# Four edits to the order of a graph kernel: weight sums, a load, attention's additions, a copy at the end

## The chip, the cores and the metric

The kernel runs on one core of a Trainium2 chip. The metric is the device time of one execution in microseconds (us), the median of several runs. Times inside an execution come from one profiled execution and count from its first instruction.

Engines are named as the profile names them: PE (TensorE) multiplies matrices, PEld is its loading of weights, DVE is VectorE, ACT is ScalarE, POOL is GpSimd, and SP is the engine that issues nearly all transfers (SyncE).

## What is computed

Two layers on x of shape (16, 1024, 256), with one adjacency matrix of 1024 x 1024, all in float32. Cut to what matters:

```python
# layer 0, per batch: attention whose queries come from a weighted adjacency
c_adj = mean over channels of x                       # (B, N)
diff  = c_adj[:, None, :] - c_adj[:, :, None]
A     = abs(abs(sigmoid(diff) - 0.5) - 0.5) * 2.0
Wg    = adj[None] * (A + transpose(A)) * 0.5
g     = relu(einsum('bcn,bnm->bcm', fea, Wg) * para)  # queries
k, v  = x @ kv_w                                      # 4 heads of 64
out   = softmax(q k^T * scale) v
x     = layernorm(x + out)
# layer 1, per batch: two graph convolutions
h = relu(x @ w1_loop + adj @ (x @ w1_neigh) + b1)
h = relu(h @ w2_loop + adj @ (h @ w2_neigh) + b2)
x = layernorm(x + (x + h) * 0.5)
```

## The kernel before

The order of all instructions is written out by hand: each engine executes its instructions in the order in which `run()` (from line 1363) issues them, and semaphores make an engine wait where data or a buffer isn't ready.

**Batches overlap.** While batch b has its attention (`Attention`), the queries of batch b+1 are prepared (`Queries`, from batch 2 on `FastQueries`), the first convolution of batch b-1 is multiplied (`c1`), and the second of batch b-2 (`c2`). From batch 2 on, the two convolutions share their products with the adjacency (`Joined`), and those, the queries and the keys use seven products of half size in place of eight, from sums of blocks that VectorE and GpSimd form beforehand. Such sums of the weights are formed once, stored to DRAM, and loaded again in each batch.

**Row buffers.** Nearly all tiles of 128 x 1024 come from one pool with the tag "row" and 31 buffers (`ROWS`, `row_tile`). The 32nd tile waits until an earlier one is read for the last time.

**The start.** `load_weights` (lines 146 to 174) loads the convolution's weights, scales them on GpSimd, forms the sums of the second layer (`w2_sums`) and then of the first (`w1_sums`), each in a row buffer, and stores them through SP. Batch 0's queries take eight rows of adjacency: `likeness(t)` computes the weight tile wg on ScalarE (lines 574 and 575), `times_adj(t)` multiplies it by the adjacency on VectorE (line 580), and `step(t)` multiplies on TensorE (line 588). In the loop over t, after row 7's weighing, VectorE also turns the next batch's x and three blocks of the adjacency (line 1406), and subtracts adjacency blocks (`adj_sums`, line 234).

**The middle of a batch, b = 2 to 14.** `att.both_units(1, ...)` computes scores (line 724) and outputs `av` (line 770) of the second pair of heads. Before its outputs, `before_convolution` puts loads on SP: `fetch("00", "10")`, two adjacency rows, `fetch(2, 3)` (four loads of 512 KB of stored adjacency sums), and `c1.load_t1()` (line 984). GpSimd then forms `both.left` (lines 1281 to 1284; from the second on they read t1) and `q.left` (lines 628 to 631).

`both.run` (from line 1293) takes the products of the joined convolutions in the order 1, 2, 6, 7, 5, 4, 3; each is eight TensorE instructions. Work of other parts is put between them: `between[n]` is issued after product n, and after product 4 behind `block_sums` (lines 1079 to 1083). Before the edit `between[1]` holds two `likeness` and `q.right(0)` (four subtractions, lines 641 to 644), `between[2]` holds `att.add_pairs(0, 1)` (denominators, lines 812 to 818, then for each pair a multiplication, an addition and a reduction, lines 821, 823 and 824, and a join of the sums), and `between[4]` two `times_adj`. VectorE's addition `uT` (line 1334) follows product 4; the last layer's small products (line 1092, `seventh_part`) need it. They come in the order 1, 2, 6, 5, 7, then the second half of product 3, then 4 and 3. VectorE's lines 1107, 1114, 1121 and 1096 take their results, and line 1357 that of product 3. Then `q.step(0)` begins on TensorE (line 669), in the PSUM banks that these results leave.

**The end.** `ending` (from line 1171) computes the last batch's second convolution tile by tile: `products` (lines 1185 and 1187), `deviations` (VectorE and GpSimd: residual, statistics, line 1196 on) and `leave` (GpSimd's lines 1204 and 1205, ScalarE's line 1207, then the store). The last quarter of the adjacency products is copied to uT by ScalarE (line 1246), behind `leave` of tile 4.

Of the kernel before, what the change touches and what calls it, by code (L numbers as in the profile page):

```python
# [18 lines left out]
def kernel(  # L19
# [126 lines left out]
    def load_weights():  # L146
        nc.sync.dma_start(out=w1l_sb, in_=w1_loop.rearrange("(cc p) f -> p cc f", p=P))
        nc.sync.dma_start(out=w1n_sb, in_=w1_neigh.rearrange("(cc p) f -> p cc f", p=P))
        nc.sync.dma_start(out=w2l_sb, in_=w2_loop)
        nc.sync.dma_start(out=w2n_sb, in_=w2_neigh)  # L150
        nc.sync.dma_start(out=b1_sb, in_=b1.rearrange("(p o) -> p o", o=1))
        nc.sync.dma_start(out=b2_sb, in_=b2.rearrange("(o f) -> o f", o=1).to_broadcast([P, C]))

        for w in (w2l_sb, w2n_sb, b2_sb):
            nc.gpsimd.tensor_scalar_mul(w, w, 1.0 / 3.0)
        for w in (w1l_sb, w1n_sb):
            nc.gpsimd.tensor_scalar_mul(w, w, LIFT)
        t = row_tile("w2_sums")
        (b11, b12), (b21, b22) = ((w[:, ts(0, P)], w[:, ts(1, P)]) for w in (w2n_sb, w2l_sb))
        t1, t2, t3, t4, b2_step = (t[:, ts(n, P)] for n in range(5))  # L160
        nc.gpsimd.tensor_sub(t1, b12, b11)
        nc.gpsimd.tensor_sub(t2, b22, t1)
        nc.gpsimd.tensor_sub(t3, b22, b12)
        nc.gpsimd.tensor_sub(t4, b21, t2)
        nc.gpsimd.tensor_sub(b2_step, b2_sb[:, ts(1, P)], b2_sb[:, ts(0, P)])
        nc.sync.dma_start(out=w2_sums, in_=t[:, 0:5 * P])
        t = row_tile("w1_sums")
        a11, a12, a21, a22 = (w[:, cc, :] for w in (w1n_sb, w1l_sb) for cc in range(NC))
        s1, s2, s3, s4 = (t[:, ts(n, P)] for n in range(4))
        nc.gpsimd.tensor_add(s1, a21, a22)  # L170
        nc.gpsimd.tensor_sub(s2, s1, a11)
        nc.gpsimd.tensor_sub(s3, a11, a21)
        nc.gpsimd.tensor_sub(s4, a12, s2)
        nc.sync.dma_start(out=w1_sums, in_=t[:, 0:FB])
# [168 lines left out]
    def by_node(t):  # L343
        return t.rearrange("p (bn r) -> p bn r", r=S)
# [351 lines left out]
    class Attention:  # L696
# [108 lines left out]
            third()  # L805

        def add_pairs(self, *pairs):
            b, half, n = self.b, FB // S, NJ * len(pairs)
            u0 = NJ * pairs[0]
            pd = bank_psum(f"den_ps_{b}_{u0}")  # L810
            den = pd[:, 0:n * NB]
            nc.tensor.matmul(den, fold.rearrange("p a k -> p (a k)"),
                             self.part[:, u0:u0 + n, :].rearrange("p u k -> p (u k)"), start=True, stop=True)
            den = den.rearrange("p (u s h) -> p u s h", u=n, s=2)
            rden = self.rden[:, u0 * half:(u0 + n) * half].rearrange("p (u h) -> p u h", u=n)
            for s in range(2):
                rows = slice(s * HD, (s + 1) * HD)
                nc.vector.reciprocal(rden[rows], den[rows, :, s, :])
            for pair in pairs:
                o = by_node(self.o.pop(NJ * pair))  # L820
                nc.vector.tensor_mul(o, o, self.rden[:, ts(pair, NB)].unsqueeze(2).to_broadcast([P, NB, S]))  # L821
                dst = by_node(self.xB[pair])
                nc.vector.tensor_add(dst, dst, o)  # L823
                nc.vector.tensor_reduce(self.sums[:, pair, :], dst, AX.X, ALU.add)  # L824
            if pairs[-1] == NC - 1:
                join(self.sums)

        def add(self, *units):
# [83 lines left out]
    class GraphConv:  # L912
# [258 lines left out]
        def ending(self, dst, quarters, aside, filled):  # L1171
# [68 lines left out]
            leave(*stats)  # L1240
            stats = deviations(4)
            products(5)
            leave(*stats)
            stats = deviations(5)
            self.neighbours(1, fourth[:, 0:half], range(TJ, NT), quarters, slice(half, FB))
            nc.scalar.copy(self.uT[:, FB + half:N], fourth[:, 0:half])
            leave(*stats)
            products(3)
            stats = deviations(3)
            leave(*stats)  # L1250
# [112 lines left out]
    def run():  # L1363
# [59 lines left out]
        for b in range(B):  # L1423
# [29 lines left out]
            if more and not c1:  # L1453
                att.both_scores(0)
                clip()
                NodeSums(q, xb, str(b + 1)).all()
                two_units(0)
                att.both_scores(1)
                for t in range(3):
                    q.load(t)  # L1460
                    q.weigh(t)
                two_units(1)
            elif more and not both:
                att.scores(0)
                att.outputs(0)
                NodeSums(q, xb, str(b + 1)).all()
                kv = KeysValues(b + 1, channel_major(blocked, f"xT_{b + 1}"))
                att.scores(1)
                kv.sums()
                att.add(0)  # L1470
                att.outputs(1)
                for t in (0, TJ):
                    q.load(t)
                c1.inner()
                q.left(nc.gpsimd)
                for t in (0, TJ):
                    q.likeness(t)
                for ij, n in QUARTERS.items():
                    store(n, quarters[ij])
                c1.first(quarters, lambda: (att.add(1), adj_sums(quarters, 1), adj_sums(quarters, 2), weigh_first()))  # L1480
                c1.turn_blocks()
                att.scores(2)
                att.outputs(2)
                for t in (1, TJ + 1):
                    q.load(t)
                    q.likeness(t)
                    q.times_adj(t)
                att.scores(3)
                for t in (2, TJ + 2, 3, TJ + 3):
                    q.load(t)  # L1490
                for t in (2, TJ + 2, 3, TJ + 3):
                    q.likeness(t)
                q.right(1)
                att.add(2)
                att.outputs(3)
            elif more:
                nodes = None

                def sums():
                    nonlocal nodes  # L1500
                    nodes = NodeSums(q, xb, str(b + 1))
                    if c3:
                        c3.squares_aside()
                    c2.load_x()
                    c1.load_inner()

                def summed():
                    c1.inner_sums()
                    if c3:
                        c3.deviation_aside()  # L1510

                def turn_next():
                    nonlocal xT_next
                    xT_next = channel_major(blocked, f"xT_{b + 1}")

                xT_next = None

                def before_convolution():
                    both.fetch("00", "10")
                    for t in (0, TJ):  # L1520
                        q.load(t)
                        q.likeness(t)
                    both.fetch(2, 3)
                    c1.load_t1()

                att.both_units(0, sums, lambda: nodes.turn(), summed=summed)
                nodes.line()
                nodes.row()
                c1.fast_inner(turn_next)
                att.both_units(1, before_convolution, third=lambda: (q.times_adj(0), q.times_adj(TJ)))  # L1530
                both.left(nc.gpsimd)
                q.left(nc.gpsimd, blocked)
                kv = KeysValues(b + 1, xT_next)
                both.fetch(1)
                for t in (1, TJ + 1):
                    q.load(t)
                both.fetch(4, "11")

                def more_weights():
                    for t in (2, TJ + 2, 3, TJ + 3):  # L1540
                        q.load(t)
                        q.likeness(t)
                    if c3:
                        c3.finish_aside(out[b - 3])

                both.run({1: (lambda: q.likeness(1), lambda: q.likeness(TJ + 1), lambda: q.right(0)),
                          2: (lambda: att.add_pairs(0, 1),),
                          4: (lambda: q.times_adj(1), lambda: q.times_adj(TJ + 1)),
                          3: (more_weights, lambda: q.right(1))},
                         last=nc.gpsimd)  # L1550
                c1.turn_blocks()
                if b + 2 < B:
                    c2.sums_aside()
            else:
                att.both_units(0, c1.load_inner, summed=c1.inner_sums)
                c1.fast_inner()
                att.both_units(1, third=lambda: att.add_pairs(0))
# [174 lines left out]
```

## Time and profile before

| | us |
|---|---|
| median of 3 runs | 2148.36 |
| lowest and highest | 2147.54 and 2150.09 |
| the profiled execution, its whole time | 2150.09 |
| the profiled execution, span from first to last instruction | 2148.3 |
| VectorE busy, of the span | 1936.7 (90%) |
| ScalarE busy | 1254.9 (58%) |
| GpSimd busy | 371.1 (17%) |

The profiled execution is itself one of the three runs, the slowest; 1.8 us of its time lie outside the span. In the views, "x8" counts instructions, a group's time is that of all of them, and in brackets stands how long the engine was idle before the group and what ended that wait. A matrix product of 512 columns in float32 is recorded as two instructions. In a windows view each line is a stretch of time, followed by its length, the busy time of PE, PEld, DVE, ACT and POOL with the number of instructions, the granted TensorE clock as a share of full speed, the share of the DMA engines and GB/s.

### The profile page before, as it was taken

The numbers are of one execution on the slowest core, as the hardware profiler recorded it, in microseconds if no ns is written. First come the engines' busy times: TensorE is split into PE (matmuls) and PEld (weight loads), VectorE is DVE, ScalarE is ACT, GpSimd is POOL, SyncE is SP. The second block draws the span as 40 slices with busy tenths as digits, with TensorE's granted clock in tenths as the row PEclk, the third lists the DMA queues.
The fourth block names the chain that finished last, engine by engine and source line by source line (L and its number), as shares of the span: only waits on it lengthen the run. The fifth ranks groups of instructions, "written<-read, shape, count | busy, mean of one in ns | idle before, by whom it ended". The sixth has DMA issues, their size and how long they took to land. (4 is left out here: it accounts for less than half of the span.)

```text
span 2148.3 us, 24753 instructions
## 1 busy us (share of the span) xinstructions
PE 2108.7 (98%) x8360; PEld 994.1 (46%) x8360; DVE 1936.7 (90%) x2212; ACT 1254.9 (58%) x2126; POOL 371.1 (17%) x224
## 2 busy tenths in 40 slices
PE   7999999999999999999999999999999999999998
PEld 4344444535444353444534445354443544445355
DVE  4899999999999899999999999999999999999885
ACT  4654564665747558465675657557475584655523
POOL 2011013122031210313102131120312103121022
PEclk9999999999999999999999999999999999999999
DMA  9388746764758657496664777647586575966454
GB/s 209 90 158 205 153 97 231 152 205 120 157 192 174 210 141 156 169 178 221 140 183 153 152 239 142 217 130 149 208 166 217 122 158 183 181 205 133 145 185 171
DMA packets 688693, 364.98 MB, mean 170 GB/s; under 512 B 550704, under 2 KB 629936, under 8 KB 688560
## 3 DMA queue, kind: packets, MB, share of 16 engines
q1 hardware_dynamic: 688288, 363.07, 65.6%
q8 instruction: 68, 1.11, 0.2%
q14 instruction: 65, 0.53, 0.1%
q10 hardware_dynamic: 272, 0.26, 0.0%
HBM read 305.46 MB, written 57.80 MB: 169 GB/s over the span
## 5 line engine op out<-in xcount | busy, mean ns | idle before, releaser
L745 DVE TENSOR_TENSOR acc<-acc,pr 128x1024 f32<-128x1024 f32 x384 | 481.1, 1253 | 34.3 <-ACT pr L731 0.9
L724 PE MATMUL s<-qT,kT 64*128 64x512 f32 x2048 | 450.8, 594 | 2.3 <-ACT qT L595 2.3
L770 PE MATMUL av<-pr,v 128*64 128x512 f32 x2048 | 447.0, 594 | 0.0
L731 ACT ACTIVATE pr<-s 128x1024 f32<-128x1024 f32 x392 | 390.8, 1115 | 41.7 <-PE s L724 40.9
L724 PEld LDWEIGHTS s<-qT,kT 64*128 64x128 f32 x2048 | 195.8, 187 | 245.0 <-issue 178.1
L770 PEld LDWEIGHTS av<-pr,v 128*64 128x64 f32 x2048 | 144.0, 137 | 297.3 <-issue 267.2
L1290 PE MATMUL hu_ps<-adj,R 128*128 128x512 f32 x480 | 213.6, 592 | 0.0
L374 POOL TENSOR_TENSOR rstd<-rstd,neg_half 128x32 f32<-128x32 f32 x16 | 88.4, 5522 | 617.2 <-DVE rstd L372 617.2
L580 DVE SCALAR_TENSOR_TENSOR wg<-wg,adj 128x1024 f32<-128x1024 f32 x128 | 170.9, 1373 | 26.7 <-ACT wg L575 26.6
L574 ACT ACTIVATE wg<-c_row,c_sums 128x1024 f32<-128x1024 f32 x120 | 139.4, 1162 | 18.9 <-DVE wg L580 17.3
L729 ACT ACTIVATE pr<-s 128x512 f32<-128x512 f32 x240 | 142.3, 702 | 0.6 <-PE s L724 0.6
L575 ACT ACTIVATE wg<-wg 128x1024 f32<-128x1024 f32 x128 | 135.4, 1057 | 4.1
L1290 PEld LDWEIGHTS hu_ps<-adj,R 128*128 128x128 f32 x480 | 89.0, 190 | 100.9 <-issue 97.8
L1290 PE MATMUL hu_ps<-adj,t 128*128 128x512 f32 x240 | 106.8, 597 | 2.8 <-DMA t<-t1d 1.8
L669 PE MATMUL g_ps<-wg,x 128*128 128x512 f32 x224 | 107.7, 593 | 0.0
L669 PE MATMUL g_ps<-T,xB 128*128 128x512 f32 x208 | 107.3, 597 | 0.0
L669 PE MATMUL g_ps<-wg,xB 128*128 128x512 f32 x208 | 106.2, 592 | 0.0
L1313 ACT COPY snap<-hu_ps 128x512 f32<-128x512 f32 x15 | 8.8, 586 | 160.6 <-PE hu_ps L1290 160.6
L1153 POOL TENSOR_TENSOR rstd<-rstd,neg_half 128x8 f32<-128x8 f32 x12 | 19.6, 1638 | 472.6 <-DVE rstd L1152 472.6
L743 DVE TENSOR_TENSOR acc<-pr,pr 128x1024 f32<-128x1024 f32 x64 | 77.9, 1217 | 21.9 <-ACT pr L731 21.9
L1281 POOL TENSOR_TENSOR R<-h 128x512 f32<-128x512 f32 x14 | 20.6, 1472 | 422.5 <-PE av L770 321.2
L752 DVE STREAM_TRANSPOSE accB<-acc 128x1024 f32<-128x1024 f32 x64 | 79.7, 1245 | 3.5 <-PE av L770 0.5
(289 smaller groups left out, 3354.8 us busy)
## 6 DMA issues: line engine op xcount, KB each, us to landing
adj<-adjT SPq DMA_DIRECT2D x210, 512.0 KB
adj<-in_adj_dram SPq DMA_DIRECT2D x128, 512.0 KB
para<-in_L_gnn_para_dram SPq DMA_DIRECT2D x32, 512.0 KB
xB_a<-in_x_dram SPq DMA_DIRECT2D x128, 128.0 KB
x1d<-xB_a SPq DMA_DIRECT2D x128, 128.0 KB
x<-x1d SPq DMA_DIRECT2D x16, 1024.0 KB
xB<-in_x_dram SPq DMA_DIRECT2D x120, 128.0 KB
x<-in_x_dram SPq DMA_DIRECT2D x15, 1024.0 KB
```

The costliest lines, as they stand in the source:

```text
L374: nc.gpsimd.tensor_tensor(self.rstd, self.rstd, neg_half, ALU.pow)
L574: nc.scalar.activation(wg, self.c_row, AF.Abs, bias=self.c_col[:, t:t + 1], scale=-1.0)
L575: nc.scalar.activation(wg, wg, AF.Tanh, scale=-0.5 / C)
L580: nc.vector.scalar_tensor_tensor(wg, wg, 1.0, self.adj.pop(t), op0=ALU.add, op1=ALU.mult)
L669: nc.tensor.matmul(self.p[n], x_n[:, k, :], w_n, start=(k == 0), stop=(k == TJ - 1))
L724: nc.tensor.matmul(halves[s], self.kT[rows, pair, ts(mt, P)], self.qT[rows, pair, ts(j, FB)], start=True, stop=True)
L729: nc.scalar.activation(pr[:, ts(s, FB)], halves[s], AF.Exp)
L731: nc.scalar.activation(pr, ps, AF.Exp)
L745: nc.vector.tensor_add(self.acc, self.acc, prs[mt])
L752: nc.vector.transpose(accB, self.acc)
L770: nc.tensor.matmul(pav[s * HD:(s + 1) * HD, :], self.v[:, mt, pair * P + s * HD:pair * P + (s + 1) * HD], prs[mt][:, ts(s, FB)], start=(mt ...
L1290: nc.tensor.matmul(dst, self.x[n][:, k, :], of_rows(rows, k), start=(start and k == 0), stop=(k == TJ - 1), skip_group_check=again)
```

## The change

1. The first layer's weight sums leave `load_weights` and become `sum_inner_weights`, called in batch 1, after two `times_adj` and before `att.scores(3)`. They are first read in batch 2.
2. In `before_convolution`, `c1.load_t1()` is issued ahead of `both.fetch(2, 3)`.
3. `add_pairs` is cut into `denominators`, `add_output` and `sum_output`. In `both.run` the denominators and pair 0's additions go after product 1, pair 0's reduction and pair 1's additions after product 2, `q.right(0)` moves from product 1 to product 6, and pair 1's reduction with the join goes after product 4, ahead of the two `times_adj`.
4. In `ending`, `leave` of tile 4 goes behind the statistics of tile 5, the adjacency products and uT's copy.

```diff
         nc.gpsimd.tensor_sub(b2_step, b2_sb[:, ts(1, P)], b2_sb[:, ts(0, P)])
         nc.sync.dma_start(out=w2_sums, in_=t[:, 0:5 * P])
+
+    def sum_inner_weights():
         t = row_tile("w1_sums")
         a11, a12, a21, a22 = (w[:, cc, :] for w in (w1n_sb, w1l_sb) for cc in range(NC))
         s1, s2, s3, s4 = (t[:, ts(n, P)] for n in range(4))
@@
         def add_pairs(self, *pairs):
+            self.denominators(*pairs)
+            for pair in pairs:
+                self.add_output(pair)
+                self.sum_output(pair)
+
+        def denominators(self, *pairs):
             b, half, n = self.b, FB // S, NJ * len(pairs)
...
-            for pair in pairs:
-                o = by_node(self.o.pop(NJ * pair))
-                nc.vector.tensor_mul(o, o, self.rden[:, ts(pair, NB)].unsqueeze(2).to_broadcast([P, NB, S]))
-                dst = by_node(self.xB[pair])
-                nc.vector.tensor_add(dst, dst, o)
-                nc.vector.tensor_reduce(self.sums[:, pair, :], dst, AX.X, ALU.add)
-            if pairs[-1] == NC - 1:
+
+        def add_output(self, pair):
+            o = by_node(self.o.pop(NJ * pair))
+            nc.vector.tensor_mul(o, o, self.rden[:, ts(pair, NB)].unsqueeze(2).to_broadcast([P, NB, S]))
+            dst = by_node(self.xB[pair])
+            nc.vector.tensor_add(dst, dst, o)
+
+        def sum_output(self, pair):
+            nc.vector.tensor_reduce(self.sums[:, pair, :], by_node(self.xB[pair]), AX.X, ALU.add)
+            if pair == NC - 1:
                 join(self.sums)
@@
             products(5)
-            leave(*stats)
-            stats = deviations(5)
+            fifth = deviations(5)
             self.neighbours(1, fourth[:, 0:half], range(TJ, NT), quarters, slice(half, FB))
             nc.scalar.copy(self.uT[:, FB + half:N], fourth[:, 0:half])
             leave(*stats)
+            leave(*fifth)
@@
+                sum_inner_weights()
                 att.scores(3)
@@
                     for t in (0, TJ):
                         q.load(t)
                         q.likeness(t)
+                    c1.load_t1()
                     both.fetch(2, 3)
-                    c1.load_t1()
@@
-                both.run({1: (lambda: q.likeness(1), lambda: q.likeness(TJ + 1), lambda: q.right(0)),
-                          2: (lambda: att.add_pairs(0, 1),),
-                          4: (lambda: q.times_adj(1), lambda: q.times_adj(TJ + 1)),
+                both.run({1: (lambda: q.likeness(1), lambda: q.likeness(TJ + 1), lambda: att.denominators(0, 1),
+                              lambda: att.add_output(0)),
+                          2: (lambda: att.sum_output(0), lambda: att.add_output(1)),
+                          6: (lambda: q.right(0),),
+                          4: (lambda: att.sum_output(1), lambda: q.times_adj(1), lambda: q.times_adj(TJ + 1)),
                           3: (more_weights, lambda: q.right(1))},
                          last=nc.gpsimd)
```

## The prediction

> **What bounds the kernel now.** I read the page's busy times first, then what TensorE waited for.
>
> ```profile
> PE 2108.7 (98%) x8360; PEld 994.1 (46%) x8360; DVE 1936.7 (90%) x2212; ACT 1254.9 (58%) x2126; POOL 371.1 (17%) x224
> ```
>
> TensorE is busy for 2108.7 of 2148.3 us, and no edit here removes one of its products. So only the 39.6 us in which it stands still, or runs at a lower clock, can be won. The list of its waits names them (total, times, longest, in us):
>
> ```profile
> PE g_ps L588 <- DVE wg L580: 13.3, 1, 13.3
> PE hu_ps L1092 <- DVE uT L1334: 7.3, 11, 1.0
> PE s L724 <- ACT qT L595: 2.3, 1, 2.3
> PE hu_ps L1290 <- DMA t<-t1d: 1.8, 3, 0.9
> PE hu_ps L1185 <- ACT uT L1246: 0.9, 1, 0.9
> ```
>
> Each edit aims at one line of it. The largest stands in batch 0. ScalarE's waits and the timeline of the first 82 us (start, length, engine, line, operation; in brackets idle time and releaser) say what is behind it:
>
> ```profile
> ACT wg L574 <- DMA w_sums<-w_sums: 22.9, 1, 22.9
> ...
> 52.59 1.15 ACT L574 ACTIVATE wg<-c_row,c_col 128x1024 f32<-128x1024 f32 x1 [22.88 <-DMA w_sums<-w_sums]
> 54.92 1.23 DVE L580 SCALAR_TENSOR_TENSOR wg<-wg,adj 128x1024 f32<-128x1024 f32 x1 [23.95 <-ACT wg L575]
> 56.20 5.60 PE L588 MATMUL g_ps<-wg,x 128*128 128x512 f32 x8 [13.29 <-DVE wg L580]
> 65.83 15.87 PE L724 MATMUL s<-qT,kT 64*128 64x512 f32 x64 [2.28 <-ACT qT L595]
> ```
>
> ScalarE's eighth weight tile wg waits 22.9 us for the store of weight sums, with which it shares no data, only a row buffer. That makes TensorE wait 13.29 us. The stages of the windows view add the clock (the number after POOL's):
>
> ```profile
> 42.90:46.40 3.50, 0.01 (x1) 0.00 (x0) 0.00 (x0) 0.00 (x0) 2.53 (x3) 1.00 0.18 48
> 46.40:56.20 9.80, 0.00 (x1) 0.00 (x1) 1.28 (x2) 2.20 (x2) 5.47 (x11) 0.50 0.39 123
> 66.00:81.60 15.60, 15.60 (x64) 6.53 (x63) 12.55 (x12) 13.42 (x19) 0.00 (x0) 0.89 0.10 38
> ```
>
> After 3.5 us without work the clock fell to half, and it fell again after the 2.28 us wait. So the stall also costs slow products: 5.60 us where eight take 8 x 0.43 = 3.44, and 15.87 where 64 score products take 13.93 elsewhere (2016.90 in the chain).
>
> The second line of the waits is in `Joined.run`, in batches 2 to 14. Batch 2 shows the wait; batch 5 doesn't, and shows the stage at its shortest:
>
> ```profile
> 366.50 0.69 DVE L1334 TENSOR_TENSOR uT<-snap,hu_ps 128x512 f32<-128x512 f32 x1
> 367.24 1.16 PE L1092 MATMUL hu_ps<-w2n_sb,uT 128*128 128x128 f32 x8 [0.74 <-DVE uT L1334]
> 375.46 1.88 PE L669 MATMUL g_ps<-wg,x 128*128 128x512 f32 x4
> ...
> 758.50 0.69 DVE L1334 TENSOR_TENSOR uT<-snap,hu_ps 128x512 f32<-128x512 f32 x1
> 764.93 0.69 DVE L1114 TENSOR_TENSOR h<-h,hu_ps 128x512 f32<-128x512 f32 x1
> 766.26 0.68 DVE L1357 TENSOR_TENSOR in<-in,hu_ps 128x512 f32<-128x512 f32 x1
> 766.72 1.06 PE L1092 MATMUL hu_ps<-w2l_sb,last 128*128 128x128 f32 x8
> 767.61 0.59 PE L669 MATMUL g_ps<-wg,x 128*128 128x512 f32 x1
> ```
>
> VectorE, not TensorE, sets the pace there: it works without a gap from the last `av` to L1357.
>
> **What the Trainium skill says.** "TensorE: Matmul & The Clock Gate", Part 1 (the HAM clock gate): the array drops to half its clock after an idle window of about 3.4 us; the trace agrees (idle from 42.9, half from 46.4). "SBUF — State Buffer", Who interferes with whom: a VectorE instruction with two SBUF inputs and a GpSimd instruction that reads SBUF block each other, a reduction doesn't. The trace agrees: L641, 0.69 by itself, took 1.75 us at 349.44 beside GpSimd's `q.left`; L823, 1.22 by itself, 2.17 at 362.82; L824 kept 1.22 at 365.02. "Perfetto Trace Analysis", Tensor Engine Instruction: VectorE, ScalarE and GpSimd run strictly in order. "DMA: Bandwidth & Descriptors", Anatomy of one DMA: a transfer's wait is served on the issuing queue, not on the DMA engines; here `t<-t1d`, issued at 335.93 behind `fetch(2, 3)`, released GpSimd only at 343.72.
>
> **Part 1, w1 sums to batch 1.** The row buffers are 31. Counted in program order, batch 0 takes 8 adj, 2 K, kv_sums, 2 para, 2 xB, 3 adjB, w2_sums, w1_sums, 4 snaps and wg 0 to 6: 31, so wg 7 is the first to reuse one. Buffers come back in the order of last use, as the wait shows: wg 7 got that of w2_sums, though adj 0 had been read by 18.2. Without w1_sums wg 7 is the 31st and waits for nothing; xB_a0, next in line, gets the buffer of w2_sums instead of w1_sums, and later tiles the same as before. wg 7 then follows wg 6 (ScalarE free at 29.7) and is multiplied by 33.2. TensorE's last product of step 6 starts at 42.32, so step 7 runs from 42.75 to 46.2, the last key and value products (1.8 us, from 61.64) to 48.0. The scores need qT. VectorE must first turn the blocked adjacency: its loads are issued to 38.8, and the weights behind them release GpSimd at 43.87, 3.5 us after their issue, so I put their arrival at 42.5. Then two transposes (3.63/6 each) to 43.7, four subtractions (2.58) to 46.3, which now run beside GpSimd's weight arithmetic: nothing to 4 x 1.06 us more (1.75 less 0.69); I take 1, so 47.3. From L599 to the first score is 1.43 us (64.40 to 65.83): 48.7, or 48.0 at best, 51.5 at worst, where the clock would also fall (1.9 us). Warm scores end at 62.6; before, the outputs began at 81.63. **Gain 19.0, bounds 19.7 and 14.2.** No later wait of batches 0 and 1 in the list stands on a transfer with a fixed time, so all behind shifts with it.
> In batch 1 the moved step issues four GpSimd operations (4 x 0.46) and one store on SP, between the adjacency loads of rows 5 and 2. It takes the buffer of the first pr of unit 2, free at about 222. Load 2, which then takes the buffer of row 1 (read until 230.7), moves from 228 to 231, and its tile is wanted at 249.7. Nothing; without that cover 3 us.
>
> **Part 2, t1 first.** t1 takes the first buffer of `fetch(2, 3)`, is issued 3.4 us earlier (-11.2 instead of -7.8 us from product 1) and lands before the first product; rows 2 and 3 are issued 0.9 us later, and product 6 wants them only 7.1 us after product 1. GpSimd's first waiting operation (L1282: 3.84 us in each of 14 runs, 53.8 in all) starts that much sooner, so fewer of its additions lie beside VectorE's.
>
> **Part 3, the additions.** VectorE's instructions are the same ones. `right(0)` goes behind product 6, the denominators' product ahead of product 2: it needs L758, which ends 1.7 us into product 1 of 3.5. Only the second pair's reduction and join (1.48 us from L824 at 365.02 to L1334 at 366.50) move past uT. So VectorE reaches uT with time in hand, and waits for product 4: uT at +21.62 as in batch 5 (times from product 1, 736.88), TensorE's wait for it is gone. But the 1.48 us are now in the queue between uT and L1114 and L1357. Batch 5 has 0.13 us of slack there, so L1114 ends at 28.73 + 1.35 = 30.09 and L1357 at 30.06 + 1.35 = 31.41. The last seventh product overwrites what L1114 reads (free at 29.84, so 0.31 us late), and step 0's first product takes the bank that L1357 reads: 31.47 instead of 30.73. What goes comes back at L1114 and L1357. Before, product 1's earliest start to step 0 took, in batches 2 to 14, 31.95, 31.46, 31.93, 31.72, 31.79, 31.63, 31.63, 31.50, 32.16, 32.55, 31.74, 31.84 and 31.35, waits for t1 included: 413.2 us. After, 13 x 31.47 = 409.1. **Parts 2 and 3: gain 4.1**; 13.7 if the waits at the tail don't come, 0 if each batch loses 0.3 more.
>
> **Part 4, the end.** uT's copy (2136.78, behind the tile that waited for GpSimd) goes ahead to 2135.65, where its product ends; the 0.87 us before L1185 at 2137.19 go, and VectorE's last tiles follow TensorE's. **Gain 0.85** (0.5 to 0.9).
>
> Sum: 19.0 + 4.1 + 0.85 = 24. The profiled execution took 2150.09 us (span 2148.3), so 2126.1; it is the slowest of three runs, and from their median, 2148.36, the forecast is **2124.4 us**.
>
> **Rivals.** (B) The tail doesn't bind, because VectorE's queue there has gaps that the trace doesn't show: 13 x 0.74 = 9.6 more, 2114.8. Against it: L1107 to L1357 follow one another without a gap in batch 5. (C) Batch 0 gets a new wait: the blocked adjacency or the contention is worse, the scores start at 51.5 or later and the clock falls again: 14 or less in place of 19, with no gain from part 3: 2133 to 2142. For it: the whole estimate rests on an arrival that no row shows. (D) The buffer isn't freed, and wg 7 waits on: 4.9, 2143.4. Against it: the count of 31. (E) Slower: the wide multiplications and additions of pair 0, moved beside GpSimd's block, are slowed. VectorE reaches uT at +22.78 in batch 2; less 1.48 that is 21.30, so slowness decides from 0.3 us on, and the kernel gets slower from 2.5 us. All four slowed by 0.95 (as L823) give 3.8: 13 x 3.5 = 45, 2170. Against it: `right(0)`, whose four took 6.7 us there instead of 2.7, leaves that block, and part 2 moves the block ahead.
>
> **How the numbers follow.** Forecast 0.64, B 0.12, C 0.16, D 0.04, E 0.04. The forecast's own bounds give 2119 to 2130; with B, and C's near end, 2115 to 2133 leaves out some 2 in 10. A measurement of this kernel tells 0.2% (4.3 us) from no change. Faster 0.94 (forecast, B, C and half of D, which lies at the bound), same 0.03 (the rest of D, a quarter of E), slower 0.03 (the rest of E).
>
> **What would show it.** L588's wait for wg and ScalarE's 22.9 us gone; scores from about 48.7 at full clock; L1334 gone from TensorE's waits, with L1114 and L1357 in its place, 0.3 to 0.5 us in each of 13 batches; t1d gone; L1246 gone. A wait of scores over 2 us, or of the denominators' product, would make it wrong.

## The result and the profile after

| | before | after |
|---|---|---|
| median, us | 2149.23 | 2123.55 |
| lowest and highest of 4 runs | 2147.54 to 2151.15 | 2122.82 to 2124.41 |
| span of the profiled execution | 2148.3 | 2122.2 |
| time after as a share of before, 95% interval | | 0.988 (0.9863 to 0.9898) |

The forecast was 2124.4 us. But what it says on the middle of a batch is right in sum only: less was lost there than forecast, and the rest was lost at another place. The lines below show both. Line numbers are those of the changed kernel; lines 574 to 802 of before stand 2 lower there, from 812 on some 8 to 14.

The busy times on the page of the changed kernel:

```profile
PE 2106.6 (99%) x8360; PEld 996.1 (47%) x8360; DVE 1884.2 (89%) x2212; ACT 1251.8 (59%) x2126; POOL 363.6 (17%) x224
```

TensorE does the same 8360 instructions in nearly the same time (2106.6 us, 2108.7 before); what lies between them fell from 39.6 to 2122.2 - 2106.6 = 15.6 us. VectorE is 52.5 us less busy with the same 2212 instructions: fewer of them lie beside GpSimd's. 48.4 of it is in the subtractions of `q.right`. The list of TensorE's waits (total, times, longest) says what is left:

```profile
PE k_ps L459 <- DMA kv_sums<-kv_sums: 2.7, 3, 1.1
PE idle L1384 <- POOL ident masks.py:199: 1.5, 1, 1.5
PE in_ps L966 <- issue: 1.3, 1, 1.3
PE hu_ps L1103 <- DVE h L1125: 0.4, 1, 0.4
```

The five lines shown of before are gone. The first line here is new: the load of the key and value weights' sums comes too late.

Batch 0, in the windows view. Before, the clock was 0.50 from 46.40 on and 0.89 in the scores:

```profile
42.90:46.40 3.50, 3.50 (x10) 1.59 (x9) 3.46 (x5) 0.00 (x0) 3.32 (x4) 1.00 0.07 20
46.40:48.60 2.20, 2.20 (x14) 1.36 (x12) 2.20 (x4) 1.23 (x2) 2.12 (x5) 1.00 0.00 0
48.60:62.50 13.90, 13.90 (x65) 6.23 (x64) 11.55 (x12) 12.74 (x17) 0.89 (x3) 1.00 0.98 183
```

and in the timeline:

```profile
32.42 1.23 DVE L582 SCALAR_TENSOR_TENSOR wg<-wg,adj 128x1024 f32<-128x1024 f32 x1 [0.90 <-ACT wg L577]
42.08 1.31 DVE L1417 STREAM_TRANSPOSE adjT<-adjB 128x512 f32<-128x512 f32 x2 [2.87 <-DMA adjB<-in_adj_dram]
43.31 3.25 DVE L236 TENSOR_TENSOR adjT<-adjT,adjT 128x512 f32<-128x512 f32 x4
48.59 14.00 PE L726 MATMUL s<-qT,kT 64*128 64x512 f32 x64
62.52 3.65 PE L772 MATMUL av<-pr,v 128*64 128x512 f32 x16
```

wg 7 is multiplied at 32.42, TensorE stays busy at full clock, and the outputs begin at 62.52 instead of 81.63: 19.1 us.

The middle stage of batch 5 (its product 1 starts at 716.80), in the timeline:

```profile
737.99 0.69 DVE L1345 TENSOR_TENSOR uT<-snap,hu_ps 128x512 f32<-128x512 f32 x1 [4.20 <-PE hu_ps L1301]
740.71 1.21 DVE L835 TENSOR_REDUCE sums<-xB_a 128x32 f32<-128x1024 f32 x1
741.95 0.19 DVE L290 TENSOR_TENSOR sums<-sums 128x32 f32<-128x32 f32 x1
745.66 0.68 DVE L1125 TENSOR_TENSOR h<-h,hu_ps 128x512 f32<-128x512 f32 x1
746.99 0.68 DVE L1368 TENSOR_TENSOR in<-in,hu_ps 128x512 f32<-128x512 f32 x1
747.70 0.72 ACT L1005 ACTIVATE h1T<-in,b_sb 128x512 f32<-128x512 f32 x1 [2.86 <-DVE in L1368]
747.72 0.30 PEld L671 LDWEIGHTS g_ps<-wg,x 128*128 128x128 f32 x2 [0.19 <-DVE in L1368]
```

VectorE has 4.20 us to spare before uT, which starts at +21.19 (times with a plus count from product 1). The moved reduction and join (L835, L290) lie between uT and L1368. L1368 ends at +30.87 and releases two things: step 0 on TensorE (+30.92) and ScalarE's relu L1005. From product 1's earliest start to step 0, waits for t1 included, the 13 batches take 401.9 us together, 413.3 before.

What waits for the relu in the end shows on SP's queue, here in batch 4 (product 1 at 585.49); an entry's length is the time that issuing takes:

```profile
629.58 0.39 SPq L1180 DMA_DIRECT2D out_dram<-x  x1
630.07 5.60 SPq L1024 DMA_DIRECT2D h1d<-h1B  x4
635.77 1.51 SPq L566 DMA_DIRECT2D para<-in_L_gnn_para_dram  x2
637.38 0.38 SPq L451 DMA_DIRECT2D kv_sums<-kv_sums  x1
```

and on TensorE, 8 us later:

```profile
645.70 1.10 PE L459 MATMUL k_ps<-K,kv_sums 128*128 128x512 f32 x2 [1.05 <-DMA kv_sums<-kv_sums]
```

ScalarE does the relu, eight operations of `likeness`, and then the scaling of an older batch's output, without a gap; SP waits for that scaling (L1180) and has the kv_sums load behind it. The period, from product 1 to the next batch's, is 130.03 us where nothing waits. Seven batches take longer, five of them with such a wait (two of 0.15 and 0.14 us are too short for the list): 130.41, 131.31, 130.41, 130.19, 131.27, 130.93 and 130.09, in sum 4.4 us more. The last period, from batch 14 to 15, is some 0.3 us longer, in e4 and e6 to e8 too, and is left out here and below.

At the end, in the timeline:

```profile
2110.73 0.37 ACT L1256 COPY uT<-u_ps 128x256 f32<-128x256 f32 x1 [0.16 <-PE u_ps L1043]
2111.39 0.59 PE L1196 MATMUL hu_ps<-w2n_sb,uT 128*128 128x256 f32 x2
```

The copy follows its product, and the last tiles' products follow the ones before them without the 0.87 us.

### The profile page after: what moved, and what is told of

Read it like the earlier page. It is cut to its first block, busy times and chain, and to the rows that moved or that the text cites. A ratio compares the mean times of both kernels' runs of the same rounds, so it can differ in the third digit from the quotient of the medians.

```text
span 2122.2 us, 24759 instructions
## 1 busy us (share of the span) xinstructions
PE 2106.6 (99%) x8360; PEld 996.1 (47%) x8360; DVE 1884.2 (89%) x2212; ACT 1251.8 (59%) x2126; POOL 363.6 (17%) x224
## 4 chain that ended last, share of the span: by engine, by line
PE 94%; DVE 3%; DMA 2%; issue 0%; SPq 0%; ACT 0%; POOL 0%; POOLq 0%; DVEq 0%
PE s L726 21%; PE av L772 20%; PE hu_ps L1301 16%; PE g_ps L671 15%; PE v_ps L463 4%; PE k_ps L459 4%; PE in_ps L966 4%; PE hu_ps L1103 4%; PE g_ps L590 2%; DMA kv_sums<-kv_sums 2%; DVE acc L747 1%; PE h_ps L1014 1%; PE u_ps L1043 1%; PE h_ps L1103 1%; PE t_ps L940 0%
```

## The experiments

All but one start from the changed kernel. "kv_sums wait" is TensorE's, from the list of waits of the profiled execution; "none" means none of 0.15 us or more.

| run | edit | median (lowest to highest), us | share of before (95%) | kv_sums wait, us |
|---|---|---|---|---|
| changed kernel | | 2123.55 (2122.82 to 2124.41) | 0.988 (0.9863 to 0.9898) | 2.7 |
| the same again | | 2124.4 (2121.32 to 2126.81) | 0.9888 (0.9872 to 0.9905) | 4.5 |
| e1 | part 1 undone | 2139.89 (2138.91 to 2143.88) | 0.9965 (0.9953 to 0.9976) | 0.9 |
| e2 | a row buffer held in the load | 2138.03 (2137.58 to 2141.18) | 0.9955 (0.9938 to 0.9973) | 2.9 |
| e3 | part 2 undone | 2125.96 (2125.34 to 2126.66) | 0.9895 (0.9878 to 0.9911) | 2.5 |
| e4 | part 3 undone | 2118.16 (2117.22 to 2119.93) | 0.9862 (0.9846 to 0.9878) | none |
| e10 | parts 2 and 3 undone | 2130.73 (2129.6 to 2132.17) | 0.9914 (0.9901 to 0.9928) | 0.8 |
| e9 | before, with part 2 alone | 2135.39 (2133.52 to 2137.81) | 0.9941 (0.9927 to 0.9954) | 1.1 |
| e5 | part 4 undone | 2122.31 (2120.66 to 2125.93) | 0.9885 (0.987 to 0.99) | 0.9 |
| e6 | second pair's sum ahead of uT | 2116.97 (2116.6 to 2118.35) | 0.9859 (0.9844 to 0.9874) | 0.2 |
| e7 | kv_sums load ahead of para | 2119.2 (2119.01 to 2119.51) | 0.9868 (0.9853 to 0.9883) | none |
| e8 | e6 and e7 together | 2115.59 (2115.32 to 2116.27) | 0.9853 (0.9836 to 0.9869) | none |

The intervals are wide because the kernel before varies by 6 us. The runs of e4, e6, e7 and e8 themselves lie apart from all eight of the changed kernel.

### Part 1: is it the buffer or the work?

e1 puts the sums back:

```diff
         load_weights()
+        sum_inner_weights()
...
-                sum_inner_weights()
                 att.scores(3)
```

> The changed kernel with the first layer's weight sums put back behind the other weight sums in the load, the rest of the change kept. Theory (part 1 is worth what the first scores show, 19.1 us, and shifts everything behind it rigidly): TensorE waits some 13 us for wg 7 in batch 0 again, the scores of unit 0 start near 67.9 us at half clock, and the time is 2123.6 + 19.1 = 2142.7 us (2141 to 2144). Rival (the gain of part 1 was partly made or lost later, for instance in the new waits for kv_sums, which depend on when batches run against the store and load queues): the time is off that by 2 us or more, with another list of kv_sums waits than 0.15, 1.05, 0.14, 1.0, 0.67.

Measured: 16.3 us slower than the changed kernel, not 19.1. The waits, and ScalarE's wg 7 in the timeline:

```profile
PE g_ps L590 <- DVE wg L582: 12.1, 1, 12.1
...
PE k_ps L459 <- DMA kv_sums<-kv_sums: 0.9, 2, 0.7
...
51.82 1.15 ACT L576 ACTIVATE wg<-c_row,c_col 128x1024 f32<-128x1024 f32 x1 [21.67 <-DMA w_sums<-w_sums]
```

The wait for wg 7 is back, 12.1 us, the clock falls (0.50 from 46.40 to 55.40, 0.89 in the scores), the scores begin at 65.06 (expected 67.9), and the outputs at 80.82, 18.3 us later. The missing part looks like the rival's: the periods of the middle batches lose 2.3 us to late data in this execution, most of it kv_sums, and 4.4 in that of the changed kernel. 18.3 - 2.1 = 16.2, beside 15.9 between the two spans. This compares one execution of each, and e1's seven runs lie up to 5.0 us apart, so it supports the rival but doesn't prove it.

e2 leaves the sums in batch 1 and takes only a buffer where they were:

```diff
         nc.sync.dma_start(out=w2_sums, in_=t[:, 0:5 * P])
+        nc.gpsimd.memset(row_tile("held")[:, 0:1], 0.0)
```

> The changed kernel with one more row buffer taken in the load of the weights, where the moved sums took theirs: GpSimd writes one column of it and nothing is stored. The sums and their store stay in batch 1. Theory (only the count of 31 row buffers matters: wg 7 is then the 32nd tile and gets the buffer of w2_sums, whose store lands late): the wait for wg 7 is back, 13 us, scores from 67.9 us, 2142.7 us (2141 to 2144). Rival (it was the arithmetic on GpSimd or the store on SP's queue that held wg 7): no wait, scores from 48.6 us, 2123.6 us.

Measured: 14.5 us slower than the changed kernel. The timeline (line numbers one higher):

```profile
48.49 0.10 POOL L167 MEMSET held<- 128x1 f32 x1
48.62 1.15 ACT L577 ACTIVATE wg<-c_row,c_col 128x1024 f32<-128x1024 f32 x1 [18.37 <-POOL held L167]
52.23 6.62 PE L591 MATMUL g_ps<-wg,x 128*128 128x512 f32 x8 [8.78 <-DVE wg L583]
```

A 32nd tile that does next to nothing brings the stall back: ScalarE waits 18.37 us for one column's write. The outputs begin at 76.30, 13.8 us later than in the changed kernel. So it is the count of 31 buffers. The size was off because wg 7 got the held tile's buffer, free as soon as GpSimd had written it. In e1, as in the kernel before, it got that of w2_sums and waited for the store issued at 49.59: wg 7 begins 3.2 us later there, of which 1.0 is that the weights came later (GpSimd begins at 43.11, in e2 at 42.10). Another 1.3 us follows in the scores, which begin after a wait of 2.3 us and take 15.83 us at a clock of 0.89, in e2 after 1.3 us and 14.51 at full clock. Together that is the 4.5 us between the two; the four subtractions of w1_sums have no part in it. By what rule a buffer is chosen stays open.

### Parts 2 and 3: each alone, both, neither

e3 and e4:

```diff
-                    c1.load_t1()
                     both.fetch(2, 3)
+                    c1.load_t1()
```

> The changed kernel with t1 loaded behind adjacency sums 2 and 3 again, the additions' new order kept. Theory (the new order has some 4 us of slack on VectorE ahead of uT, so the later GpSimd block costs nothing there, and part 2 alone is worth only TensorE's waits for t1, 3.3 us over 13 batches before): GpSimd starts at 0 from product 1 and ends near 12, right(0) ends by 19, uT stays at 21.2, time 2126 to 2128 us. Rival (it is the earlier block that takes the contention off VectorE; without it uT is late again by 0.7 us a batch): uT at 21.9 or later, 2133 us or more.

```diff
-                both.run({1: (..., lambda: att.denominators(0, 1), lambda: att.add_output(0)),
-                          2: (lambda: att.sum_output(0), lambda: att.add_output(1)),
-                          6: (lambda: q.right(0),),
-                          4: (lambda: att.sum_output(1), ...),
+                both.run({1: (..., lambda: q.right(0)),
+                          2: (lambda: att.add_pairs(0, 1),),
+                          4: (...),
```

> The changed kernel with right(0) ahead of the additions again and both pairs added behind product 2, as before; t1 stays ahead. Theory (the GpSimd block now ends at 9.0 instead of 12 us, so right(0) ends by 10.5 instead of 12.5, and VectorE reaches uT by 21.2 all the same; the second pair's sum lies ahead of uT, so step 0 is at 30.73 instead of 30.91): no wait for uT, step 0 at 30.7 to 30.8, time 2120 to 2124 us: the new order would then be worth nothing beside part 2. Rival (the order is what removed the wait): uT at 22.3 or later, TensorE waits 0.3 to 0.7 us a batch for it, 2129 to 2134 us.

e10 makes both edits, e9 makes part 2's in the kernel before:

> The changed kernel with both part 2 and part 3 undone: only the weight sums' move and the copy at the end are left. With it, parts 2 and 3 are known alone and together. Theory (either of the two takes the waits for uT away, so they are worth less together than apart, and the sum behind uT costs some 5 us only where uT is in time already): uT waits of 7 us and t1 waits of 2 us are back, time 2129 to 2132 us, so that part 3 alone gains 3 to 6 us, while beside part 2 it loses 5.4. Rival (part 3 costs what it costs, with or without part 2): 2126.0 - 5.4 = 2120.6 us.

> The kernel before with nothing but part 2: t1 loaded ahead of adjacency sums 2 and 3. Theory (the earlier GpSimd block alone takes away TensorE's waits for uT and for t1): product 1 to step 0 takes 399.9 us over 13 batches instead of 413.3, uT at 21.2 to 21.5, and the time is 2148.5 - 13.4 = 2135.1 us (2133.5 to 2137). Rival (part 2 frees uT only together with the rest of the change, or new waits for kv_sums come as in the changed kernel): 2139 us or more.

With parts 1 and 4 in place, the medians make a square:

| us | old order of additions | new order (part 3) |
|---|---|---|
| t1 behind | 2130.73 | 2125.96 |
| t1 first (part 2) | 2118.16 | 2123.55 |

The runs are not all from one chip; beside them the kernel before had medians of 2148.5 to 2149.2, so a difference of 1 us in the square means little. Part 3 gains 4.8 us without part 2 and loses 5.4 beside it. Part 2 gains 12.6 alone, and 2.4 beside part 3. In the kernel before, part 2 alone is worth 12.8 (2148.18, the median before on that chip, to 2135.39; expected 13.4). Either edit takes away the waits for uT; only part 2 takes away those for t1 as well; only part 3 puts something new behind uT.

In e10 both waits are back:

```profile
PE hu_ps L1103 <- DVE uT L1345: 5.5, 9, 0.7
PE hu_ps L1301 <- DMA t<-t1d: 2.7, 3, 1.5
```

e3, in batch 9 (product 1 at 1239.84), shows how the new order frees uT although t1 is late. GpSimd begins 0.04 us after product 1 and is still at work at 1252.54; VectorE's `right(0)` ends at 1257.53 and uT, at +21.15, waits for TensorE alone:

```profile
1239.88 1.27 POOL L1293 TENSOR_TENSOR R<-R,t 128x512 f32<-128x512 f32 x1 [3.62 <-DMA t<-t1d]
1251.27 1.27 POOL L633 TENSOR_TENSOR xB<-x,xB 128x512 f32<-128x512 f32 x1
1256.84 0.69 DVE L646 TENSOR_TENSOR T<-wg,T 128x512 f32<-128x512 f32 x1
1260.99 0.69 DVE L1345 TENSOR_TENSOR uT<-snap,hu_ps 128x512 f32<-128x512 f32 x1 [3.46 <-PE hu_ps L1301]
```

e4, in batch 5 (product 1 at 714.46), shows how t1 first frees it in the old order:

```profile
719.96 1.75 DVE L643 TENSOR_TENSOR T<-wg 128x512 f32<-128x512 f32 x1
724.02 0.69 DVE L646 TENSOR_TENSOR T<-wg,T 128x512 f32<-128x512 f32 x1
735.64 0.69 DVE L1345 TENSOR_TENSOR uT<-snap,hu_ps 128x512 f32<-128x512 f32 x1 [1.51 <-PE hu_ps L1301]
743.87 0.68 DVE L1368 TENSOR_TENSOR in<-in,hu_ps 128x512 f32<-128x512 f32 x1
```

Two of `right(0)`'s subtractions still take 1.7 us beside GpSimd, the other two 0.69: GpSimd's block has ended by then. uT is at +21.18, with 1.51 us to spare and the second pair's sum already done. So L1368 ends at +30.09, 0.77 earlier than in the changed kernel, and step 0 starts at +30.76. kv_sums is issued at +51.0 instead of +51.8, and no period lasts longer than 130.07. The expectation missed that second gain: it stopped at step 0.

### What the sum behind uT costs, and the load

e6 moves the one sum; e7 moves the one load; e8 does both:

```diff
-                          6: (lambda: q.right(0),),
-                          4: (lambda: att.sum_output(1), lambda: q.times_adj(1), ...),
+                          6: (lambda: q.right(0), lambda: att.sum_output(1)),
+                          4: (lambda: q.times_adj(1), ...),
...
-                q.load_para()
                 kv.load()
+                q.load_para()
                 q.step(3, lambda: norm.variance(bank_psum), 4)
```

> The changed kernel with the second pair's sum and join moved from behind uT to behind right(0), where VectorE idles some 4 us; all else as in the change. Theory (what the new order costs is only this sum behind uT: L1368 ends at 30.86 instead of 30.09, so step 0 starts 0.15 us late and ScalarE's relu, eight likeness operations, the output store, the h1d stores and the kv_sums load all come 0.77 us late): step 0 at 30.76, kv_sums issued at 51.0 instead of 51.8, no TensorE wait for it, period 129.77, time as with the old order, 2118.2 us (2117 to 2119.5). Rival (another part of the new order costs, such as the additions beside GpSimd's block): some of it stays, 2121 us or more.

> The changed kernel with the kv_sums load issued ahead of the two para loads in the middle batches; the second pair's sum stays behind uT. Theory (kv_sums lands just too late because it is issued too late): issued at 50.2 instead of 51.8, no TensorE wait for it, period 130.03 in every batch, time 2123.55 - 4.4 = 2119.2 us (2118 to 2120.5). Rival (the load's landing is set by what else is on the DMA queues, not by its place): waits of the same size, 2123 us or more; or para comes late in its place and VectorE's scaling, then the scores, wait: over 2124 us.

> The changed kernel with both edits: the second pair's sum behind right(0), and the kv_sums load ahead of the para loads. Theory (the sum ahead takes 0.26 us off each period, the load ahead takes away what is left of the kv_sums waits, some 0.8 us in the run with the sum ahead alone): period 129.76 in all middle batches, no wait for kv_sums, time 2116.97 - 0.8 = 2116.2 us (2115.5 to 2117). Rival (the two edits do the same thing twice, and what was left over there was not the load): 2117 us.

All three came out as the theory had it, e6 and e8 by 1.2 and 0.6 us below the number expected. SP's queue in batch 4, of e6 (product 1 at 584.42):

```profile
633.87 1.40 SPq L566 DMA_DIRECT2D para<-in_L_gnn_para_dram  x2
635.31 0.43 SPq L451 DMA_DIRECT2D kv_sums<-kv_sums  x1
```

and of e7 (584.40):

```profile
634.65 0.62 SPq L451 DMA_DIRECT2D kv_sums<-kv_sums  x1
635.31 1.21 SPq L566 DMA_DIRECT2D para<-in_L_gnn_para_dram  x2
```

In e6 both loads come 0.8 to 1.0 us earlier than in the changed kernel; in e7 kv_sums alone, by 1.6, and L1368 stays at +30.86. e7's period is 130.02 or 130.03 in each batch, which is the changed kernel without its waits; e8's is 129.76 or 129.77. The difference, 0.26, is what the sum behind uT costs directly: 0.16 at step 0's start (+30.91 and +30.75), and 0.10 between its first two products. Over 13 batches that is 3.4 us, the waits for kv_sums another 4.4 in the profiled execution. On the same chip, e8 is 8.8 us below the changed kernel and 32.9 below the kernel before: it beats both.

### Does the wait for kv_sums belong to certain batches?

The changed kernel was profiled again.

> The changed kernel once more, beside the combined version on the same chip. Theory (kv_sums lands so close to its use that the other traffic decides in which batches TensorE waits): the same 30.91 and 130.03, the waits for kv_sums in other batches than 3, 4, 5, 7 and 8, in sum 1 to 5 us, time 2121.5 to 2124.5 us. Rival (the waits are tied to certain batches): the same list of waits.

It waited for kv_sums in batches 5 to 9 and 14 (in batch 4 the list names a tile of VectorE's), the first execution in 3, 4, 5, 7 and 8. Product 1 to step 0 is 30.91 in both. So the waits don't belong to certain batches: the load lands so near to its use that small differences decide. That these come from the other traffic is likely, but not shown. The sum of the waits (2.7, then 4.5 us) varies as well and may be a part of the changed kernel's spread; e7 and e8, without them, keep within 0.5 and 0.95 us.

### Part 4

```diff
             stats = deviations(4)
             products(5)
-            fifth = deviations(5)
+            leave(*stats)
+            stats = deviations(5)
...
-            leave(*stats)
-            leave(*fifth)
+            leave(*stats)
```

> The changed kernel with uT's last copy at the end behind the fifth tile's scaling again. Theory (part 4 is worth the gap that it closes): TensorE waits about 0.9 us for uT ahead of its last products, time 2123.55 + 0.85 = 2124.4 us. Rival (the last tiles' statistics and stores set the end, not TensorE): the gap is back and the time is unchanged at 2123.5 us.

The median can't tell: the run is 1.2 us below the changed kernel's, with less waiting for kv_sums in its profile. The timeline can:

```profile
2109.44 0.35 ACT L1257 COPY uT<-u_ps 128x256 f32<-128x256 f32 x1
2109.84 0.70 PE L1196 MATMUL hu_ps<-w2n_sb,uT 128*128 128x256 f32 x2 [0.85 <-ACT uT L1257]
```

The gap is back. From the start of the last adjacency products to the end of the span it takes 2120.5 - 2106.24 = 14.3 us, in the changed kernel 2122.2 - 2108.80 = 13.4.

## Why the prediction was right, and where it was not

**Part 1 was right, step by step.** The buffer was the cause (e2), wg 7 waits for nothing, and the gain of 19.0 is 19.1 in the trace. Two errors inside it made up for each other. VectorE's part ended early: the adjacency arrived at 42.08, not 42.5, and the four subtractions took 3.25 us beside GpSimd (2.58 alone, 3.58 forecast), so they ended at 46.56 instead of 47.3. TensorE's part ended late: the last key product began at 46.74, not 46.2. So it is TensorE's own work that sets the scores' start at 48.59, not VectorE's, as the forecast had it.

**Parts 2 and 3: the mechanism was right, the size was not.** That TensorE's wait for uT goes, and that L1368 then releases step 0 late, is what the trace shows. The term that was mis-sized is VectorE's slack behind uT. The forecast took uT's time, +21.62, and 0.13 us of slack from batch 5 of the kernel before, on the reading that uT waited for product 4 there. It did not, as the timeline of before shows:

```profile
757.16 1.26 POOL L1079 TENSOR_TENSOR last<-h1T,uT 128x512 f32<-128x512 f32 x1
757.24 1.23 DVE L288 TENSOR_TENSOR sums<-sums 128x32 f32<-128x32 f32 x1
```

The join of the sums, 0.19 us in 11 of 13 batches, took 1.23 us beside a GpSimd addition, and ended at 758.47; uT began at 758.50 behind it. (Batch 9, the other one with uT so early, shows the same.) Freed of that, uT starts 0.44 us earlier, at +21.18. L1368 ends at 30.09 in e4, and at 30.86 with 1.48 us of work put ahead of it: the slack is 1.48 - 0.77 = 0.71, not 0.13. Step 0 comes 0.16 us late instead of 0.74, and of the waits forecast at L1114 and L1357 (now L1125 and L1368) in every batch none is on the list, but for one of 0.4 us that stood there before. Nor did VectorE work without a gap in that stage, as the forecast says: in batch 5 of before it was idle for 0.87 us at 742.31 and 0.20 at 746.68. So the stage gained 11.4 us, not 4.1, near rival B's 13.7.

**What took it back was not in the forecast.** It followed L1368 to step 0 and stopped there. The same lateness of 0.77 us runs on through ScalarE and SP to the kv_sums load, which had little slack, and made a new wait there: 4.4 us. From the load's issue to the moment when TensorE is ready for it there are 7.2 us in the changed kernel (median of batches 3 to 14), 7.7 in the kernel before and in e6, 8.8 in e7; where TensorE waited for it, in the two executions of the changed kernel, it came 6.8 to 8.7 us after its issue. The kernel before issued it no earlier, at some +52.0, but needed it later too. And this much isn't safe either: e9 has 7.8 us, and waits 1.1. Rival C looked for a new wait in batch 0; this one is in the middle batches. e6, e7 and e8 show the chain. The sum over the spans: 19.1 + 11.4 + 0.9 - 4.4 - 13 x 0.10 (between step 0's first two products) = 25.7, of 26.1 measured. So that the forecast's 24 was near is luck in the middle batches: two errors of opposite sign, 7.3 and some 5.7, cancelled.

**Which edit did it** the forecast left open, giving parts 2 and 3 one sum. It put the end of the uT wait down to part 3's order. The square shows that part 2 does it alone, and that part 3, beside it, costs more than it brings. Rival E, which had part 3's additions slowed beside GpSimd, is close in kind but not in place: L832 does take 2.18 us there (e3 and the changed kernel), and VectorE still has 3.5 to 4.2 us to spare before uT.

**Part 4** was right: 0.85 forecast, a gap of 0.85 in e5's trace and 0.9 over the tail. **Rival D**, that the buffer isn't freed, fell with the wait itself.

## What to carry to other kernels

When two edits aim at the same wait, run each alone and both: here the cheaper one did all of it, and the other only moved work to where there was no slack. Follow a delayed instruction to everything that it releases, also over engines that aren't the bottleneck: 0.77 us on VectorE went through ScalarE's order and SP's queue and came out as TensorE's wait some 28 us later. And where a pool of buffers has just as many tiles as the code takes, one more tile that does nothing can cost most of what the work that it stands for costs: 13.8 of 18.3 us here.

## What the runs showed of the hardware

- A very small VectorE instruction can be held for nearly the whole of a GpSimd instruction. The join of 128x32 took 0.19 us alone and 1.23 beside a GpSimd addition of 1.26, and ended 0.05 us after it. In e4's batch 5 it began late in such an addition, took 0.34, and again ended 0.05 us after it. The Trainium skill ("SBUF — State Buffer", Who interferes with whom) names the kind: a VectorE instruction with two SBUF inputs against a GpSimd instruction that reads SBUF. The traces agree, also in that the reduction L835 kept its 1.21 us beside GpSimd (e3, at 1250.82).
- Of two such instructions the one that begins second waits. In the changed kernel's batch 5 a VectorE multiplication begins 0.02 us before a GpSimd addition and keeps its 1.22 us; the addition takes 2.34 instead of 1.27. The next VectorE instruction, which begins within that addition, takes 2.18 instead of 1.22:

```profile
723.46 1.22 DVE L830 TENSOR_TENSOR o<-o,rden 128x1024 f32<-128x1024 f32 x1
723.47 2.34 POOL L633 TENSOR_TENSOR xB<-x,xB 128x512 f32<-128x512 f32 x1
724.71 2.18 DVE L832 TENSOR_TENSOR xB_a<-xB_a,o 128x1024 f32<-128x1024 f32 x1
```

- A wait of TensorE lengthens the period by more than the idle time that the profile shows for it. The waits for kv_sums of 0.15, 1.05, 0.14, 1.00 and 0.67 us lengthened it by 0.38, 1.28, 0.38, 1.24 and 0.90: 0.23 to 0.24 more each time. 0.16 of that is a matter of the records: the small products ahead of the wait are recorded as 0.27 us long but follow one another every 0.11 us, so the idle time is counted from an end that is 0.16 late. The other 0.07: behind a wait the first two products take 1.10 us together instead of 1.02. Why they do is open.
